# Two old sums fed later: P5 of a blocked matrix product collected in fresh buffers

## The chip, the cores and the metric

One core of one Trainium2 chip runs the whole program. The metric is the device time of one execution in microseconds (us). Before the change it is 2571.3 us, the median of 3 runs (2570.91 to 2572.54). PE is the matrix engine (TensorE), DVE the vector engine, ACT the scalar engine, POOL GpSimd, and SP the engine that only issues DMAs. ACT and POOL issue DMAs too, on queues of their own.

## The reference, cut to what matters

The input x holds 32 items of 128 rows and 2048 features. Of the first layer the part that matters here is one big product: all 4096 rows times one 2048 x 2048 weight (which has the low-rank update already in it). The mixing of an item's 128 rows by its own 128 x 128 matrix, an average of 8 matrices by attention weights, commutes with it and comes after.

```python
agg_w = jnp.einsum('bk,koi->boi', att, weight[..., 0])
out   = jnp.einsum('boi,bih->boh', agg_w, x) + agg_b[:, :, None]
...
out = jnp.einsum('bsd,od->bso', x, W) + bias
upd = jnp.einsum('ebsr,eor,e->bso', einsum('bsd,erd->ebsr', x, A), Bf, coeffs * scales)
x = x + out + upd
```

The second layer (a grouped convolution, a feature permutation, a gated network for each of 16 heads and its inverse permutation) fills the second half of the time and is not touched.

## The kernel before, in words

**The product in three levels.** The big product is done by Strassen's scheme in Winograd's form: a product of 2 x 2 blocks is made of seven products of sums instead of eight. The outer level has the seven rounds `P1, P2, P6, P7, P5, P3, P4`, in this order (`ROUNDS`). A round goes over 8 groups of 4 items, `g` = 0 to 7, so there are 56 steps `(r, g)`, numbered 0 to 55; P5 is steps 32 to 39 and P3 steps 40 to 47. Inside a step the seven products of the second level are again named P1 to P7. One of them is 4 matmuls of 128 x 128 weights and 512 columns that accumulate in one PSUM bank; each 32-bit matmul stands in the trace as two MATMUL records.

**The third level** takes two neighbouring groups (a pair, `PAIRS`) together: for the inner products P2 and P4 of both, 16 matmuls of 512 columns become 28 of 256 (`quarter` in `multiply_third`, all in the odd step of the pair). In the pairs that `MORE` lists, P3 and P7 are done so as well (`multiply_more`, where the first two quarters of each family are in the even step). The weights of the third level are made by POOL and DVE (`third_weights`, `more_weights`), its inputs by POOL or DVE (`third_inputs`: `sq`; `more_inputs`: `sv`).

**What becomes of a product.** A round's products belong to one or two sums in DRAM (`ADDED`). P5 goes to two: `u1` becomes `u3` and `u2` becomes `c11`. `olds_load` loads the old sums one step ahead, DVE adds each PSUM bank to the loaded tile as soon as PE has filled it (`add`, line 600 and line 506; `quarter`, lines 628, 538 and 543), and `part_store` stores the tile from SP's queue after the pair. So in P5 DVE reads each bank twice, once for each sum. Where there is no old sum (P1), the first write to each part of a fresh tile `m_` is a copy by ACT (line 602), and the later ones are DVE's additions.

**What sets the order.** The schedule is written by hand: an engine runs its instructions in the order of the Python calls. `between(j)`, called between the products of a step, puts side work on DVE: `mixed_kernel` (the averages of 8 matrices, lines 725 and 727; `MIXES[r][g]` of them at each of j = 0 to 3), parts of third-level weights (lines 1319 and 1321). Loads of the round's inputs (`x_loads`) and of the next round's weights (`outer_weights`) stand on SP's queue; SP waits, in order, until the place of a load is free, and everything behind that load waits too. POOL makes the sums of inputs (`x_combine`: `pieces`, line 292, then `s`, lines 328 to 331) and, at the end of a round, the next round's inner weights (`inner_weights`, lines 261 to 265).

**Buffers.** All large tiles (128 x 2048, 1 MB) share 26 places (`SLOTS`). A new tile takes a place that another one has left, and the first instruction that writes to it waits for the last one that used the place, which may be a store on another queue. PSUM has 8 banks; a product takes `px` or `py` and reuses it two products later, so PE waits if the bank has not been emptied by then.

Of the kernel before, what the change touches and what calls it, by code (L numbers as in the profile page):

```python
# [11 lines left out]
ALU = mybir.AluOpType  # L12
# [4 lines left out]
P = 128  # L17
B = 32
L = 2048
QW = 512  # L20
# [31 lines left out]
    "P1": (0, 1, 2, 3), "P2": (0, 1, 2, 3), "P6": (0, 1, 2, 3), "P7": (0, 1, 2, 3),  # L52
    "P5": (0, 1, 2, 3), "P3": (0, 1, 2, 3), "P4": (0,),
}
MORE = {"P6": (1,), "P7": (1, 2, 3), "P3": (1, 2, 3)}
MIXES = {
# [6 lines left out]
    "P4": (0,) * 8,  # L63
}
ENDS = ("P1", "P4")
# [4 lines left out]
def adaln_ffn_kernel(  # L70
# [16 lines left out]
    nc = tc.nc  # L87
# [8 lines left out]
    def slot(name, shape=(P, L)):  # L96
        return big.tile(list(shape), FP, name=name, tag="s")


    def bank():  # L100
        return banks.pop(0)
# [178 lines left out]
    def part_load(n, g, shape=(P, 2, 2, QW)):  # L280
        t = slot(f"{n}_{g}", shape)
        nc.sync.dma_start(t.rearrange("p k s c -> p (k s c)"), part_d[n, g])
        return t

    def part_store(n, g, t, eng=nc.gpsimd):
        eng.dma_start(part_d[n, g], t.rearrange("p k s c -> p (k s c)"))
# [30 lines left out]
    def x_combine(r, g, ts):  # L317
# [22 lines left out]
    ADDED = {  # L340
        "P1": [(None, "p1")],
        "P2": [("p1", "c00")],
        "P6": [("p1", "u1")],
        "P7": [("u1", "u2")],
        "P5": [("u1", "u3"), ("u2", "c11")],
        "P4": [("u2", "c10")],
        "P3": [("u3", "c01")],
    }
# [144 lines left out]
    def multiply_more(r, g, lhs, rhs, accs, between, families):  # L493

        px, py = bank(), bank()
        if g % 2 == 0:
            both = [accs]
            held.extend((both, {}, {}))
        both, *sums = held
        if g % 2:  # L500
            both.append(accs)

        def add(ps, *to):
            for si, oi in to:
                for acc in accs:
                    nc.vector.tensor_tensor(acc[:, si, oi], ps, acc[:, si, oi], ALU.add)

        def product(k, ps, first, last):
            for kc in range(4):
                nc.tensor.matmul(  # L510
                    ps, lhsT=lhs[k][:, bass.ts(kc, P)], rhs=rhs[k][kc],
                    start=first and kc == 0, stop=last and kc == 3, skip_group_check=True,
                )

        def quarter(n, k):

            quarters, x = families[n]
            qs = sums[n]
            if k in ("P1", "P5", "P2"):
                qs[k] = bank()  # L520
            ps = qs[{"P6": "P1", "P7": "P1", "P4": "P1", "P3": "P5"}.get(k, k)]
            first, last = k in ("P1", "P2", "P5"), k in ("P2", "P3", "P4")
            for i, out in enumerate(halves(ps)):
                for kc in range(2):
                    nc.tensor.matmul(
                        out, lhsT=x[k][:, 1 - i if n else i, bass.ts(kc, P)],
                        rhs=quarters[i][k][kc],
                        start=first and i == 0 and kc == 0, stop=last and i == 1 and kc == 1,
                        skip_group_check=True,
                    )  # L530
            b, h = {
                "P1": (0, 0), "P2": (0, 0), "P6": (0, 1), "P5": (1, 1), "P7": (1, 1),
                "P3": (0, 1), "P4": (1, 0),
            }[k]
            cols = slice(h * NQ, (h + 1) * NQ)
            for acc in both[b]:
                part = acc[:, :, n, cols]
                nc.vector.tensor_tensor(
                    part, ps.rearrange("p (s n) -> p s n", s=2), part, ALU.add
                )  # L540
                if n:
                    part = acc[:, 1, 0, cols]
                    nc.vector.tensor_tensor(part, ps[:, NQ : 2 * NQ], part, ALU.add)
            if last:
                done(ps)

        def quarters_of(*nks):
            if g % 2:
                for n, k in nks:
                    quarter(n, k)  # L550

        product("P1", px, True, False)
        add(px, (0, 0))
        between(0)
        quarters_of((0, "P6"), (0, "P5"))
        if g % 2:
            sums_rest(nc.vector)
        product("P5", py, True, True)
        add(py, (1, 1), (0, 1))
        done(py)  # L560
        between(1)
        quarters_of((1, "P6"), (0, "P7"))
        product("P6", px, False, True)
        add(px, (0, 1), (1, 1), (1, 0))
        done(px)
        between(2)
        if g % 2 == 0:
            quarter(0, "P1")
            quarter(0, "P2")
            between(3)  # L570
            quarter(1, "P1")
            between(4)
            quarter(1, "P2")
            between(5)
            return
        quarters_of((1, "P5"), (0, "P3"))
        between(3)
        quarters_of((1, "P7"), (0, "P4"))
        between(4)
        quarters_of((1, "P3"))  # L580
        between(5)
        quarters_of((1, "P4"))
        held.clear()
        for b, accs in enumerate(both):
            for (_, new), acc in zip(ADDED[r], accs):
                part_store(new, g - 1 + b, acc, nc.sync)

    def multiply_third(r, g, lhs, rhs, olds, between, quarters, sq):

        px, py = bank(), bank()  # L590
        accs = olds if olds[0] is not None else [slot(f"m_{r}{g}", (P, 2, 2, QW))]
        fresh = set()
        if sq:
            both = [held.pop(), accs]
# [47 lines left out]
                for k, to in turns[n]:  # L642
                    quarter(k, to)

        early = r not in ENDS
        product("P1", px, True, False)
        add(0, 0, px)
        between(0)
# [26 lines left out]
        if not sq:  # L675
            held.append(accs)
            return
        for b, accs in enumerate(both):
            for (_, new), acc in zip(ADDED[r], accs):
                part_store(new, g - 1 + b, acc, nc.scalar if r == "P1" else nc.sync)  # L680

    held = []

    def outer_weights(r, kc):

# [499 lines left out]
    steps = [(r, g) for r in ROUNDS for g in range(NG)]  # L1185
# [40 lines left out]
    olds = {}  # L1226
# [4 lines left out]

    def olds_load(i):
        r, g = steps[i]
        olds[i] = [old and part_load(old, g) for old, _ in ADDED[r]]

    for i, (r, g) in enumerate(steps):
        ri = i // NG
# [18 lines left out]
            olds_load(0)  # L1256
        if i + 1 < len(steps) and not last_round and i != NG - 1:
            olds_load(i + 1)
        ahead = i + 2 < len(steps) and ri > 0 and not last_round
        if ahead and steps[i + 2][0] != "P6":  # L1260
            xs[i + 2] = x_loads(*steps[i + 2])
        if g == NG - (1 if ri else 2) and ri < len(ROUNDS) - 1:
            nxt = inner_weights(ROUNDS[ri + 1], [nxt[kc] for kc in range(4)])
# [40 lines left out]
        def between(j):  # L1304

            if j == 3 and 0 <= k_early < EARLY:
                outer_sums(k_early, early_x)

            b = (ri - 1) * (NG - 2) + g + 1 if ri > 0 else g - (NG - 2)
            if j < 4:  # L1310
                for _ in range(MIXES[r][g]):
                    if mixes:
                        b, k = mixes.pop(0)
                        mixed_kernel(b, (k,))
            if ri == 0 and j == 2:
                for k in blocks[6 + 2 * g : 8 + 2 * g]:
                    wt[k] = w_load(*k)
            if i and j < 4 and quarter_ops:
                nc.vector.tensor_tensor(*quarter_ops.pop(0), ALU.subtract)
            if j < 4 and more_ops:  # L1320
                nc.vector.tensor_tensor(*more_ops.pop(0), ALU.subtract)
            if i == NG - 1 and j == 3:
                olds_load(i + 1)
            if j == 3 and ahead and steps[i + 2][0] == "P6":
                xs[i + 2] = x_loads(*steps[i + 2])
            if ri == 0 and unsummed and (j in (1, 3) and (i, j) != (1, 3) or (i, j) == (3, 2)):
                row_sums(*unsummed.pop())
            if (i, j) in ((2, 5), (3, 0), (3, 4), (4, 0)) and unsummed_first:
                t = unsummed_first.pop(0)
                tt = nc.vector.tensor_tensor  # L1330
                tt(wsum[:, 0, 0], wsum[:, 0, 0], t[:, 0, 0], ALU.add)
                tt(wsum[:, 0], wsum[:, 0], t[:, 1], ALU.add)
            if last_round:
                if j == 1 and i + 1 < len(steps):
                    lhs[i + 1] = x_combine(*steps[i + 1], xs.pop(i + 1))
                    olds_load(i + 1)
                if j == 4 and i + 2 < len(steps):
                    xs[i + 2] = x_loads(*steps[i + 2])
                if j in (2, 4):
                    stage(k0 + j // 2, stage_first)  # L1340
                if j % 2:
                    stage_third(k0 + j // 2)
                else:
                    stage(k0 + j // 2, stage_second)
# [116 lines left out]
```

## Time and profile before

| what | value |
|---|---|
| median of 3 runs | 2571.3 us |
| the profiled execution, by the same clock as the runs | 2569.07 us |
| its span in the profile | 2567.3 us |
| PE busy in the span | 2556.8 us |
| first matmul after the span's start | 1.5 us |
| last matmul's end before the span's end | 5.8 us |
| P5, steps 32 to 39 | 848.5 to 1034.2 us |
| P3, steps 40 to 47 | 1034.2 to 1216.0 us |
| granted TensorE clock | 1.00 |

The profile is a table of what each engine did in one execution. The page sums it up; the timeline lists instructions in order of time, with the idle time ahead of each group in brackets and what ended it; the windows view gives the busy time of each engine in a stretch; the waits view says who waited for whom. A busy PE is not PE at its peak, since matmuls overlap: the distance from one matmul's start to the next is the better measure. The start of a step is the start of its first matmul. Times in the profile count from the start of the span.

### The profile page before, as it was taken

What the parts mean: (1) busy time and instruction counts of PE and PEld (TensorE: products, weight loads), DVE (VectorE), ACT (ScalarE), POOL (GpSimd) and SP (SyncE); (2) the same over time, 40 slices, a digit from 0 to 9 for tenths busy, and PEclk for the clock granted to TensorE, in tenths of its full rate; (3) what the DMA queues carried; (4) which work ended last, traced back from release to release, by engine and by line L of the source; (5) the groups of instructions that cost most, each with busy time, mean ns of one, the idle gap of its engine ahead of it and who ended that gap; (6) DMA issues with size and microseconds to landing.
All of it is one profiled execution on the core that took longest, in us unless ns stands there. A gap on an engine that the chain in (4) does not pass through costs nothing. (4 is left out here: it accounts for less than half of the span.)

```text
span 2567.3 us, 22404 instructions
## 1 busy us (share of the span) xinstructions
PE 2556.8 (100%) x7238; PEld 1373.6 (54%) x7238; DVE 1616.1 (63%) x2505; ACT 532.2 (21%) x1099; POOL 1411.2 (55%) x1170
## 2 busy tenths in 40 slices
PE   9999999999999999999999999999999999999999
PEld 4555555565566555566554455455554554455543
DVE  5575566777776658766477666666666666666601
ACT  0000000000000000000011344444444444444432
POOL 8433677879997836989532144434334434434222
PEclk9999999999999999999999999999999999999999
DMA  8553688569466586574876987777777787787532
GB/s 344 195 187 117 242 322 313 210 267 392 150 248 265 202 340 264 230 287 165 285 237 202 298 297 248 224 251 235 230 218 239 246 251 222 222 250 239 163 125 90
DMA packets 186868, 610.44 MB, mean 238 GB/s; under 512 B 17664, under 2 KB 91904, under 8 KB 142336
## 3 DMA queue, kind: packets, MB, share of 16 engines
q1 hardware_dynamic: 146784, 465.09, 51.0%
q0 software_dynamic: 31264, 119.56, 14.1%
q10 hardware_dynamic: 8704, 24.37, 2.5%
q8 instruction: 58, 0.95, 0.1%
q14 instruction: 58, 0.48, 0.1%
HBM read 372.45 MB, written 202.94 MB: 224 GB/s over the span
## 5 line engine op out<-in xcount | busy, mean ns | idle before, releaser
L999 PE MATMUL bank<-t,ws 128*128 128x512 f32 x1024 | 460.3, 592 | 0.0
L1010 PE MATMUL bank<-gl,ws 128*128 128x512 f32 x1024 | 460.2, 592 | 0.0
L1017 POOL DMA_INDIRECT out<-t,orow x128 | 151.3, 1182 | 545.5 <-DVE t L1015 488.1
L1002 ACT ACTIVATE gl<-bank 128x512 f32<-128x512 f32 x512 | 306.2, 598 | 433.1 <-PE bank L999 430.6
L1010 PEld LDWEIGHTS bank<-gl,ws 128*128 128x128 f32 x1024 | 194.6, 190 | 233.0 <-issue 231.5
L999 PEld LDWEIGHTS bank<-t,ws 128*128 128x128 f32 x1024 | 194.6, 190 | 226.6 <-issue 223.4
L1015 DVE TENSOR_TENSOR t<-bank,t 128x512 f32<-128x512 f32 x128 | 88.4, 690 | 322.0 <-PE bank L1010 322.0
L748 POOL TENSOR_TENSOR x<-x,fb 128x512 f32<-128x512 f32 x128 | 174.2, 1390 | 182.8 <-DMA x<-in_x 133.8
L754 ACT ACTIVATE bank<-w,aggb 128x512 f32<-128x512 f32 x128 | 80.8, 684 | 877.5 <-DMA w<-w_d 865.3
L607 PE MATMUL bank<-P_t,s_P 128*128 128x512 f32 x576 | 255.7, 592 | 0.4 <-ACT m_P L602 0.4
L292 POOL TENSOR_TENSOR xt<-xt,xt 128x512 f32<-128x512 f32 x120 | 156.3, 1334 | 97.7 <-DMA xt<-in_xT 78.8
L727 DVE SCALAR_TENSOR_TENSOR ags<-mix,att_bc,ags 128x128 f32<-128x128 f32 x224 | 200.1, 893 | 4.2
L607 PEld LDWEIGHTS bank<-P_t,s_P 128*128 128x128 f32 x576 | 109.3, 190 | 127.6 <-issue 122.2
L328 POOL TENSOR_TENSOR s_P<-xt 128x512 f32<-128x512 f32 x52 | 68.8, 1323 | 191.4 <-DMA xt<-in_xT 110.3
L983 POOL DMA_INDIRECT t<-hx_d,row x128 | 131.5, 1027 | 54.4 <-issue 25.6
L600 DVE TENSOR_TENSOR u<-bank,u 128x512 f32<-128x512 f32 x132 | 85.3, 685 | 101.9 <-PE bank L607 98.9
L607 PE MATMUL bank<-wo_P,s_P 128*128 128x512 f32 x320 | 142.1, 592 | 0.0
L866 ACT ACTIVATE cv<-bank,ctxb 128x128 f32<-128x128 f32 x256 | 73.0, 368 | 233.4 <-PE bank L855 233.4
L855 PE MATMUL bank<-va,tw_l 128*128 128x256 f32 x512 | 121.1, 379 | 0.0
L766 DVE TENSOR_TENSOR x<-bank,x 128x512 f32<-128x512 f32 x128 | 88.0, 690 | 52.4 <-PE bank L763 21.5
L855 PEld LDWEIGHTS bank<-va,tw_l 128*128 128x128 f32 x512 | 97.0, 190 | 40.9 <-issue 30.5
L600 DVE TENSOR_TENSOR p<-bank,p 128x512 f32<-128x512 f32 x84 | 56.6, 687 | 96.5 <-PE bank L607 94.1
(239 smaller groups left out, 4030.1 us busy)
## 6 DMA issues: line engine op xcount, KB each, us to landing
xt<-in_xT SPq DMA_DIRECT2D x84, 1024.0 KB, 10.3
u<-u_d SPq DMA_DIRECT2D x40, 1024.0 KB, 9.6
wo_P<-wb_d SPq DMA_DIRECT2D x36, 1024.0 KB, 12.3
u<-c_d SPq DMA_DIRECT2D x64, 512.0 KB, 7.0
x<-in_x SPq DMA_DIRECT2D x32, 1024.0 KB, 8.9
xg<-x SPq DMA_DIRECT2D x256, 128.0 KB, 5.1
hx_d<-x1t SPq DMA_DIRECT2D x32, 1024.0 KB, 6.6
hx_d<-ht SPq DMA_DIRECT2D x32, 1024.0 KB, 7.2
```

The lines of the kernel that those rows point to most:

```text
L292: nc.gpsimd.tensor_tensor(out[:, i, j], a[:, i, j], b[:, i, j], op)
L600: nc.vector.tensor_tensor(to, ps, to, ALU.add)
L607: nc.tensor.matmul(ps, lhsT=lhs[k][:, bass.ts(kc, P)], rhs=rhs[k][kc], start=first and kc == 0, stop=last and kc == 3, skip_group_check=True,)
L727: nc.vector.scalar_tensor_tensor(ag, mix[:, k], att, ag, ALU.mult, ALU.add)
L748: nc.gpsimd.tensor_tensor(xt[:, f], xt[:, f], late["fb"][:, f], ALU.add)
L855: nc.tensor.matmul(out, lhsT=w[:, 2 * i + r], rhs=rhs, start=first and r == 0, stop=last and r == 1, skip_group_check=True,)
L983: nc.gpsimd.indirect_dma_start(out=t.rearrange("p k t -> p (k t)"), out_offset=None, in_=hx_d[g].rearrange("l k t -> l (k t)"), in_offset= ...
L999: nc.tensor.matmul(pu, lhsT=w[:, m * P : (m + 1) * P], rhs=t[:, 0], start=True, stop=True)
L1002: nc.scalar.activation(gl[m], pu, AF.Gelu)
L1010: nc.tensor.matmul(pd, lhsT=w[:, (MC + m) * P : (MC + m + 1) * P], rhs=gl[m], start=(m == 0), stop=(m == MC - 1),)
L1015: nc.vector.tensor_tensor(t[:, 1], pd, t[:, 1], ALU.add)
L1017: nc.gpsimd.indirect_dma_start(out=out, out_offset=bass.IndirectOffsetOnAxis(ap=orow[:, g, h : h + 1], axis=0), in_=t[:, 1], in_offset=None,)
```

## The change

P5's results of groups 0 to 5 (three pairs) no longer go to two loaded sums. They are collected in one fresh tile `m_P5g` for each group (first writes by ACT, the others by DVE), and that tile is kept in SBUF. In the next two steps its old sums are loaded and DVE adds the tile to each of them, in halves of 1024 columns at j = 2 to 5 of `between` (line 1345 of the new file, below called a fold); the sums are then stored from ACT's queue. Groups 6 and 7 still go to both sums directly, as before. Pair 1 of P5 (groups 2 and 3) gets the third level for P3 and P7 as well. In a fresh pair the quarters of the odd step come after the products that write the fresh tile first. Loads of P5's inputs are issued later, at j = 3 instead of ahead of the step; P1's stores go from ACT's queue to SP's, but for pair 2; one or two of `MIXES` move between steps, so that P5 has 28 averaging operations instead of 32, and P3 48 instead of 44.

```diff
-MORE = {"P6": (1,), "P7": (1, 2, 3), "P3": (1, 2, 3)}
+MORE = {"P6": (1,), "P7": (1, 2, 3), "P3": (1, 2, 3), "P5": (1,)}
-    "P5": (0, 0, 0, 1, 1, 2, 2, 2),
-    "P3": (0, 2, 1, 2, 1, 2, 2, 1),
+    "P5": (0, 1, 0, 1, 0, 1, 2, 2),
+    "P3": (0, 2, 1, 2, 1, 2, 2, 2),
...
     def multiply_more(r, g, lhs, rhs, accs, between, families):
         px, py = bank(), bank()
+        fresh = accs[0] is None
+        early = not fresh
+        if fresh:
+            accs = [slot(f"m_{r}{g}", (P, 2, 2, QW))]
+        untouched = [(si, oi) for si in range(2) for oi in range(2)] if fresh else []
...
                 for acc in accs:
-                    nc.vector.tensor_tensor(acc[:, si, oi], ps, acc[:, si, oi], ALU.add)
+                    if (si, oi) in untouched:
+                        untouched.remove((si, oi))
+                        nc.scalar.copy(acc[:, si, oi], ps)
+                    else:
+                        nc.vector.tensor_tensor(acc[:, si, oi], ps, acc[:, si, oi], ALU.add)
...
-        quarters_of((0, "P6"), (0, "P5"))
+        quarters_of((0, "P6"), (0, "P5"), now=early)
...
-        quarters_of((1, "P6"), (0, "P7"))
+        quarters_of((1, "P6"), (0, "P7"), now=early)
...
+        quarters_of((0, "P6"), (0, "P5"), (0, "P7"), now=fresh)
+        quarters_of((1, "P6"), now=fresh)
         quarters_of((1, "P5"), (0, "P3"))
...
+        if fresh:
+            folds.extend((g - 1 + b, accs[0]) for b, accs in enumerate(both))
+            return
...
     def multiply_third(r, g, lhs, rhs, olds, between, quarters, sq):
-        early = r not in ENDS
+        early = r not in ENDS and olds[0] is not None
...
+        if r == "P5" and olds[0] is None:
+            folds.extend((g - 1 + b, accs[0]) for b, accs in enumerate(both))
+            return
-                part_store(new, g - 1 + b, acc, nc.scalar if r == "P1" else nc.sync)
+                part_store(new, g - 1 + b, acc, nc.scalar if (r, g) == ("P1", 5) else nc.sync)
...
     def olds_load(i):
-        olds[i] = [old and part_load(old, g) for old, _ in ADDED[r]]
+        olds[i] = [None] if r == "P5" and g < 6 else [old and part_load(old, g) for old, _ in ADDED[r]]
...
+        fold = folds.pop(0) if folds else None
+        if fold:
+            fold += ([part_load(old, fold[0]) for old, _ in ADDED["P5"]],)
         ahead = i + 2 < len(steps) and ri > 0 and not last_round
-        if ahead and steps[i + 2][0] != "P6":
+        if ahead and steps[i + 2][0] not in ("P6", "P5"):
             xs[i + 2] = x_loads(*steps[i + 2])
...
+            if fold and j > 1:
+                n, si = divmod(j - 2, 2)
+                t = fold[2][n]
+                nc.vector.tensor_tensor(t[:, si], t[:, si], fold[1][:, si], ALU.add)
+                if si:
+                    part_store(ADDED["P5"][n][1], fold[0], t, nc.scalar)
...
-            if j == 3 and ahead and steps[i + 2][0] == "P6":
+            if j == 3 and ahead and steps[i + 2][0] in ("P6", "P5"):
                 xs[i + 2] = x_loads(*steps[i + 2])
```

More of the change, by code (lines that the diff above doesn't have):

```diff
@@ L545, in quarter, with quarters_of @@
                 done(ps)
-        def quarters_of(*nks):
-            if g % 2:
+        def quarters_of(*nks, now=True):
+            if g % 2 and now:
                 for n, k in nks:
@@ L677, in multiply_third @@
             return
+        if r == "P5" and olds[0] is None:
+            folds.extend((g - 1 + b, accs[0]) for b, accs in enumerate(both))
+            return
         for b, accs in enumerate(both):
             for (_, new), acc in zip(ADDED[r], accs):
-                part_store(new, g - 1 + b, acc, nc.scalar if r == "P1" else nc.sync)
-    held = []
+                part_store(new, g - 1 + b, acc, nc.scalar if (r, g) == ("P1", 5) else nc.sync)
+    held, folds = [], []
     def outer_weights(r, kc):
```

## The prediction

> **What bounds the kernel now.** I read the page's busy line first, then who PE waits for, then the timeline of PE in P5, and last the busy time step by step. The busy line of the page:
>
> ```profile
> PE 2556.8 (100%) x7238; PEld 1373.6 (54%) x7238; DVE 1616.1 (63%) x2505; ACT 532.2 (21%) x1099; POOL 1411.2 (55%) x1170
> ```
>
> PE is busy nearly throughout. Overlapping matmuls also look busy, so the waits of PE are the next view (us in total, times, longest):
>
> ```profile
> PE bank L166 <- DVE warm L163: 1.5, 1, 1.5
> PE bank L232 <- DVE w L235: 1.3, 1, 1.3
> PE bank L525 <- DVE u L543: 1.0, 2, 0.5
> PE bank L525 <- DVE p L543: 0.4, 1, 0.4
> PE bank L607 <- ACT m_P L602: 0.4, 1, 0.4
> ```
>
> Only three of the five lines are in the rounds, 1.8 us in 2567; line 525 appears where pairs with `MORE` write two sums. Measured on the starts of neighbouring matmuls, all pauses of the run come to 6.4 us, and P5 has none. The timeline of PE in step 34 gives the beat (start, us, operation, count of records):
>
> ```profile
> 894.91 3.60 PE L607 MATMUL bank<-wo_P,xt 128*128 128x512 f32 x8
> 898.34 7.03 PE L607 MATMUL bank<-P_t,s_P 128*128 128x512 f32 x16
> ...
> 922.39 3.62 PE L620 MATMUL bank<-P_q,sq 128*128 128x256 f32 x16
> 925.85 3.60 PE L607 MATMUL bank<-P_t,s_P 128*128 128x512 f32 x8
> ```
>
> From 894.91 to 898.34 are 8 records, so 0.429 us each; a 512-column matmul (two records) costs 0.858 us. Sixteen records of 256 columns fill 922.39 to 925.85, so such a matmul costs 0.432. The busy time in steps 36 to 40 (one line each; per engine):
>
> ```profile
> core 0: us, PE busy (x) PEld busy (x) DVE busy (x) ACT busy (x) POOL busy (x), PEclk, DMA share, GB/s
> 941.30:958.40 17.10, 17.10 (x41) 7.60 (x40) 8.61 (x16) 0.00 (x0) 1.99 (x2) 1.00 0.84 328
> 958.40:987.70 29.30, 29.30 (x97) 18.24 (x96) 25.45 (x34) 0.00 (x0) 22.93 (x19) 1.00 0.75 313
> 987.70:1004.90 17.20, 17.20 (x41) 7.60 (x40) 10.01 (x20) 0.00 (x0) 2.12 (x2) 1.00 0.84 327
> 1004.90:1034.10 29.20, 29.20 (x97) 18.24 (x96) 24.36 (x34) 0.00 (x0) 23.91 (x19) 1.00 0.51 208
> 1034.10:1051.30 17.20, 17.20 (x41) 7.60 (x40) 9.73 (x13) 0.00 (x0) 16.96 (x14) 1.00 0.73 258
> ```
>
> DVE has half of an even step free, but only 4 to 5 us of an odd one. The DMA share is high in steps 36 to 38.
>
> **PE's own work.** Pair 1 of P5 turns 16 matmuls of 512 columns into 28 of 256: 16 x 0.858 - 28 x 0.432 = 13.7 - 12.1, **-1.6 us**. PE is the bound, so this is saved in full if nothing comes late.
>
> **DVE's relief.** Six groups lose their second addition (0.69 us by the row of line 600 below). PE waits for none of them, so this buys **0**. In their place come 24 folds of 1024 columns in SBUF. Their nearest row is line 252:
>
> ```profile
> L252 DVE TENSOR_TENSOR wsum<-wsum,w 128x1024 f32<-128x1024 f32 x24 | 34.6, 1440 | 0.5
> L600 DVE TENSOR_TENSOR u<-bank,u 128x512 f32<-128x512 f32 x132 | 85.3, 685 | 101.9 <-PE bank L607 98.9
> ```
>
> Its shortest is 1.21 us and its longest 2.28. A mix of line 727 takes 0.35 us while POOL rests (999.8 us) and 1.24 while POOL works (1009.8), so I take 1.7 for a fold beside POOL and 1.3 otherwise.
>
> A rule of the Trainium skill (VectorE: DVE Perf Modes, The TRN2 errata) gives such an fp32 addition as (N+151)/0.96 ns, an estimate of 1.22 us for 1024 columns. The shortest row agrees, the mean of 1.44 does not; by the rule the folds named below would end about 0.9 us earlier and the stall of step 37 be 4.4 us instead of 5.4.
>
> **Step 35 (the new `MORE` step).** Ten quarters stand in a row, with folds and mixes on DVE between the evictions. A quarter needs the bank emptied two quarters before; behind two additions, a mix and a fold (about 0.4 + 0.4 + 1.2 + 1.7) one quarter comes some 0.3 late, and later ones like the stalls of line 525 in P3 and P7 (0.2 to 0.7). **+0.7**, between 0 (DVE keeps up, as in P5 now) and 2 (a fold at 2.28 in each of three such places).
>
> **Step 37, where I expect most of it.** Its fresh tile `m_P55` gets the place of `c11`'s sum of group 2 (`u2` loaded in step 36). The last user of that place is the store, now on ACT's queue, that follows the fold at j = 5 of step 36. ACT's first copy into `m_P55` therefore waits for the landing. In the times of before, where step 37 starts at 958.5, and now 1.6 - 0.7 = 0.9 earlier, at 957.6:
> - DVE has added the last bank of step 36 at 957.6 + 0.7 = 958.3, and does the two folds left, 2 x 1.7: 961.7.
> - The store lands. Before, line 286 shows six 1 MB stores from ACT's queue, landing after 3.9 / 10.1 / 12.3 us (least, median, most). At step 37's start SP issues the two loads of 1 MB for the next fold. A second 1 MB transfer of a burst lands 2.1 to 2.5 us after the first, so with one and a half of them mixed in: 3.9 + 1.5 x 2.4 = 7.5. Landing 969.2.
> - The copy, 0.59 to 0.7 with its wake-up: 969.9.
> - PE's third product (P6) takes the bank of the first again two products after the step's start: 957.6 + 16 x 0.429 = 964.5.
>
> So PE stands for **+5.4**. Lower end: folds of 1.2 and a landing in 3.9 give 958.3 + 2.4 + 3.9 + 0.7 = 965.3, 0.8 us. Upper end: a landing in 12.3 gives 10.2. Behind the waiting copy ACT has the other copies and the stores of the next folds; DVE waits for the bank too, so the whole step moves. The other fresh tiles of the even and odd steps have the same kind of predecessor, but 1 us or more to spare by the same working (`m_P54` about 4, `m_P53` about 1): 0, or up to 2, which the upper end covers.
>
> A rule that speaks against this edit is in DMA: Bandwidth & Descriptors, Queues, rings and completion order: an engine goes round-robin between queue rows, so ACT's store would share with SP's loads rather than pass them. The rows of 10.1 and 12.3 us agree; half of 425 GB/s for 1 MB and the page's fixed 2 us make an estimate of 7 us, and the sum would be 0.5 less.
>
> **Steps 38 to 40.** Groups 6 and 7 are still added twice, and the folds of groups 4 and 5 now come on top: step 38 has 10.0 + 4 x 1.4 = 15.6 of 17.2 us, or with POOL's overlap up to 19; step 39 has 24.4 + 4 x 1.5 = 30.4 of 29.3, and mixes that move there. DVE then enters P3 some 8 us behind at worst, and the third product of step 40 waits for the eviction of the first, about 1.9. A second path ends at the same place: P3's inner weights (lines 261 to 265, POOL) need places that a fold's store now frees. `P3_t1` had 4.8 us to spare, `P3_q0` 2.7, `s_P31` 6.1, and the load of `s2_0` stands on SP behind a store from ACT; by these the weights come 0.2 us late. Both are one wait, not two: **+2.0**, between 0 (folds at 1.2 and additions kept inside the free 5 us) and 4 (the backlog and the late load one behind the other).
>
> **The rest.** P3's group 7 has four more mixes, 4 x 0.9 on a DVE that makes line 525 wait: **+0.3**, between 0 and 1.2. The later loads of P5's inputs take from a margin of 20 us before POOL needs them: 0, or at most 1. P1's stores pass to SP's queue, where SP is ahead of their readers by 30 us: 0; should loads stand behind them it is a stall of P1 like that of line 602, 0.4. Four mixes less in P5: 0, DVE has free time there.
>
> **Sum.** -1.6 + 0.7 + 5.4 + 2.0 + 0.3 = **+6.8 us**. Against the profiled execution's own 2569.07 us (span 2567.3) that is 2575.9; it stands 2.2 below the median, so on the median of 2571.3 I forecast **2578.1**.
>
> **Rivals.**
> 1. *Not slower: the store lands alone* (2571.5). If SP's two loads are themselves held by an occupied place, nothing shares the transfers; the store takes 3.9, step 37 loses 0.8, and the rest 1.0 (half of step 35, a third of P3's start): 2571.3 - 1.6 + 0.8 + 1.0. For it: the least row, 3.9, and the fact that the 26 places are all taken. Against: a DMA share of 0.84. It decides once the landing takes under about 5.8 us, since then the whole is below the 5.1 us that count.
> 2. *Only PE's count shows* (2569.7): the folds fit the gaps of DVE (0.95 to 1.74 us in its timeline of step 38) and the store's place is free in time; the relief of DVE does nothing, because PE did not wait for it. For it: no stall in P5 now. Against: odd steps have only 4 to 5 us free.
> 3. *Much slower* (2584): step 37 at its upper end, 10.2 - 5.4 = 4.8 more, and 1 more at P3's start.
> 4. *Faster*: would need the 1.6 and most of the 6.4 us of all pauses, of which only one kind (0.4 at P1's copy) touches what is edited: at best 2563.
>
> **Chances.** Forecast mechanism from 2576.4 up to 2582: 0.42; rival 3: 0.08; rival 1: 0.31; rival 2: 0.17; rival 4: 0.02. Differences of under 0.2% (5.1 us) are about what a measurement of this kernel can't tell from no change. So slower by more than that 0.50, the same 0.48, faster 0.02. The range runs from rival 2 (2569.4, with its 0.3 of scatter) to rival 3 (2586, its mechanism with 2 us of the other fresh tiles), leaving out about 1 in 10.
>
> **What would show it.** Right: 7 to 10 us of new pauses of PE, most of it one wait for ACT's first copy (line 513 or 616 of the new file) at the start of step 37, with a landing of 6 to 10 us in the row of the folds' stores (line 286), and a smaller one in the first products of P3. The distance from step 34 to 36 should shrink by 1.6 less any stall. Wrong: no wait for ACT at step 37 with landings near 4 (rival 1 or 2); a stall in P1 or elsewhere in P2 to P7, which I cost at nothing; folds of 1.2 us beside POOL, which take away the terms of steps 35 and 40.

## The result, and the profile after

The changed kernel takes **2581.57 us** (median of 6, 2580.89 to 2583.44) against 2571.11 for the kernel before (median of 6): ratio 1.0043, 95% interval 1.0033 to 1.0053, so 10.5 us slower. The profiled execution took 2580.89 us with a span of 2578.7, 11.4 more than the 2567.3 of before. The forecast was 2578.1 with a range of 2569.4 to 2586.0.

The page's busy line, and then who PE waited for (us in total, times, longest), in the changed kernel (line 513 or 616 is ACT's first copy, 534 a quarter of the third level, 621 a product):

```profile
PE 2559.4 (99%) x7262; PEld 1378.7 (53%) x7262; DVE 1625.7 (63%) x2470; ACT 545.9 (21%) x1123; POOL 1443.3 (56%) x1182
```

```profile
PE bank L621 <- POOL P_t L261: 5.4, 2, 3.3
PE bank L621 <- ACT m_P L616: 3.2, 3, 2.1
PE bank L534 <- DVE u L552: 1.6, 2, 0.9
...
PE bank L519 <- ACT m_P L513: 0.6, 1, 0.6
```

The busy line hides it all: PE is at 99% instead of 100%. The waits show three new ones in P5 and P3 (0.4 of the 3.2 is P1's copy, as before), and the largest is not the one that the forecast put first: 5.4 us for POOL's sums for P3's inner weights. Worked out as before, on the starts of neighbouring matmuls:

| part | us |
|---|---|
| 16 matmuls of 512 columns become 28 of 256 | -1.6 |
| step 35: third product 0.9, one quarter 0.3 | +1.2 |
| step 36, third product | +0.9 |
| step 37, third product | +2.3 |
| step 40, second product of P3: two waits 6.2, then matmuls at half speed 3.2 | +9.4 |
| the pause at 178 us is gone | -1.5 |
| new small pauses at 353 us (0.3) and 1413 us (0.9, layer two) | +1.2 |
| sum, against 11.4 in the span | +11.9 |

What the sum has too much lies in small pauses that are not listed: one of 0.4 us at 756 us is gone, the start is 0.2 us shorter, and one at 800 us is 0.2 us longer.

The steps say the same: from the start of step 34 to that of step 36 it took 46.42 us before and 45.98 now (-1.6 + 1.2), step 37 took 29.26 and now 31.56, step 40 took 17.16 and now 26.62.

**Steps 35 to 37.** The timeline of ACT in the changed kernel (start, us, operation; in brackets the idle time ahead and what ended it):

```profile
916.83 0.33 ACTq L286 DMA_DIRECT2D c_d<-u  x1
917.26 1.56 ACT L513 COPY m_P<-bank 128x512 f32<-128x512 f32 x3 [11.64 <-DVE ags L742]
...
946.09 1.07 ACT L616 COPY m_P<-bank 128x512 f32<-128x512 f32 x2 [22.41 <-DMA u_d<-u]
...
961.45 0.33 ACTq L286 DMA_DIRECT2D c_d<-u  x1
965.56 1.07 ACT L616 COPY m_P<-bank 128x512 f32<-128x512 f32 x2 [6.86 <-DMA c_d<-u]
```

The last two lines are the predicted wait of step 37: the store of `c11`'s sum of group 2 is issued at 961.45, lands 4.0 us later, and the copy into `m_P55` starts 0.1 us after that. In step 36 it is the same with the store of group 1's first sum, which landed 9.8 us after its issue. In step 35 the copy starts right behind the issue of a store on ACT itself.

**P3's start.** The timeline of SP's queue in the changed kernel:

```profile
1015.47 0.32 SPq L282 DMA_DIRECT2D s<-s_d  x1
```

The same load in the kernel before:

```profile
994.67 0.65 SPq L282 DMA_DIRECT2D s<-s_d  x1
```

What POOL waited for between 1000 and 1050 us in the changed kernel:

```profile
POOL xt L292 <- DMA s<-s_d: 17.1, 1, 17.1
```

The load of `s2_0`, which P3's first step needs, was issued at 994.67 before and now at 1015.47: its place is that of `u1`'s old sum of group 4, whose store went out at 1007.75 and landed at 1015.33. POOL stood still for 17.1 us until the load landed (18.6 us before, where the load came sooner), began P3's sums at 1020.59 (1008.46 before) and then had all of P3's inner weights to make. The timeline of PE shows the price, and the windows the clock:

```profile
1038.61 1.88 PE L621 MATMUL bank<-P_t,s_P 128*128 128x512 f32 x4
1043.78 2.07 PE L621 MATMUL bank<-P_t,s_P 128*128 128x512 f32 x2 [3.29 <-POOL P_t L261]
1048.00 7.09 PE L621 MATMUL bank<-P_t,s_P 128*128 128x512 f32 x10 [2.15 <-POOL P_t L261]
```

```profile
core 0: us, PE busy (x) PEld busy (x) DVE busy (x) ACT busy (x) POOL busy (x), PEclk, DMA share, GB/s
1043.00:1048.00 5.00, 2.07 (x2) 0.50 (x2) 1.27 (x2) 0.00 (x0) 4.79 (x4) 0.50 1.01 397
1048.00:1053.00 5.00, 5.00 (x6) 2.17 (x7) 2.29 (x2) 0.00 (x0) 4.89 (x4) 0.50 1.01 411
```

The third part of the weights comes 3.3 us late and the fourth 2.2 us more; after the first wait the granted clock is 0.50 in these windows, and a record takes 0.85 us instead of 0.43. POOL, too, was slower than before while it made them (lines of POOL, then of DVE):

```profile
1034.40 2.33 POOL L263 TENSOR_TENSOR P_t<-wo_P,P_t 128x512 f32<-128x512 f32 x1
```

```profile
1034.39 1.21 DVE L1345 TENSOR_TENSOR u<-u,m_P 128x1024 f32<-128x1024 f32 x1
```

A sum of POOL that starts together with a fold of DVE takes 2.33 us instead of 1.27. From the start of POOL's chain to the weights' fourth part it took 27.4 us (24.4 before); four such sums beside folds and one beside line 1339 make 4.3 of it (before, POOL also waited 1.1 us in this stretch). The Trainium skill (SBUF — State Buffer, Who interferes with whom) says that a DVE instruction with two SBUF inputs and a GpSimd instruction that reads SBUF exclude each other, the later one waiting for the earlier. The rows agree: 2.33 is 1.27 and most of a fold's 1.21.

### The profile page after: what moved, and what is told of

It reads as the page before. It is cut to its first block, busy times and chain, and to the rows that moved or that the text cites. A ratio compares the mean times of both kernels' runs of the same rounds, so it can differ in the third digit from the quotient of the medians.

```text
span 2578.7 us, 22472 instructions
## 1 busy us (share of the span) xinstructions
PE 2559.4 (99%) x7262; PEld 1378.7 (53%) x7262; DVE 1625.7 (63%) x2470; ACT 545.9 (21%) x1123; POOL 1443.3 (56%) x1182
## 5 line engine op out<-in xcount | busy, mean ns | idle before, releaser
L621 PE MATMUL bank<-P_t,s_P 128*128 128x512 f32 x544 | 245.5, 600 | 8.6 <-POOL P_t L261 5.4
L744 DVE SCALAR_TENSOR_TENSOR ags<-mix,att_bc,ags 128x128 f32<-128x128 f32 x224 | 212.6, 949 | 4.3
L616 ACT COPY m_P<-bank 128x512 f32<-128x512 f32 x48 | 27.8, 586 | 757.6 <-PE bank L621 626.9
L621 PEld LDWEIGHTS bank<-P_t,s_P 128*128 128x128 f32 x544 | 104.1, 192 | 134.2 <-issue 120.0
L621 PE MATMUL bank<-wo_P,s_P 128*128 128x512 f32 x288 | 127.5, 592 | 0.0
L780 PE MATMUL bank<-u,agl 128*128 128x512 f32 x256 | 115.1, 592 | 0.0
```

The source lines that it names most:

```text
L621: nc.tensor.matmul(ps, lhsT=lhs[k][:, bass.ts(kc, P)], rhs=rhs[k][kc], start=first and kc == 0, stop=last and kc == 3, skip_group_check=True,)
L744: nc.vector.scalar_tensor_tensor(ag, mix[:, k], att, ag, ALU.mult, ALU.add)
L780: nc.tensor.matmul(pm, lhsT=ag, rhs=u[:, f], start=False, stop=True, skip_group_check=True)
```

## The experiments

Each ran beside the kernel before on the same chip. The median of before was 2571.08 for experiments 1 to 4, 2571.01 for 5 to 8 and 2570.35 for 9 to 12. In the diffs "..." stands for lines left out, and a line in round brackets for several lines that it sums up.

**1. Pair 2 directly**

```diff
-        olds[i] = [None] if r == "P5" and g < 6 else ...
+        olds[i] = [None] if r == "P5" and g < 4 else ...
```

> The changed kernel, but groups 4 and 5 go directly to both old sums again, as groups 6 and 7 do; groups 0 to 3 stay fresh. Theory A (the folds of groups 4 and 5 and their stores from ACT's queue cause the wait at step 37 and the late start of P3): the pause of 2.2 us at step 37's third product and the 9.4 us in the first products of P3 both go, the pauses in steps 35 and 36 (1.2 and 0.9) stay: 2581.6 - 11.7 = 2569.9 us. Theory B (the later loads of P5's inputs and the moved mixes delay POOL, the folds do not): P3's pause stays at 7 us or more, 2577 to 2580 us.

Measured: 2585.51 us, ratio 1.0055 (1.0041 to 1.0069). The two pauses did go (none in step 37's third product, 1.1 us left at P3's start), as theory A said. But PE had lost 13 us by then, which gave POOL time as well, so this run alone does not show that the folds of groups 4 and 5 made them, and theory B is not ruled out by it; experiments 5, 8, 10 and 12 bear on that. The new pause of 13.2 us, slow matmuls behind it included, stands in step 35, and smaller ones in steps 37, 39 and 41 (0.7, 1.5 and 1.8). Step 35, PE, then ACT, each from its own timeline:

```profile
931.12 6.25 PE L519 MATMUL bank<-P_t,s_P 128*128 128x512 f32 x8 [10.39 <-ACT m_P L513]
```

```profile
920.24 0.36 ACTq L286 DMA_DIRECT2D c_d<-u  x1
930.39 1.56 ACT L513 COPY m_P<-bank 128x512 f32<-128x512 f32 x3 [21.39 <-DMA c_d<-u]
```

The old sums of group 4, now loaded here, took two places, and the fresh tile `m_P53` got the place of a sum whose store was just going out; among the loads it took 10 us to land. It is the predicted mechanism of step 37 at its upper end, in another step. My expectation had counted the places as they were; when one tile goes, the others get other places.

**2. and 4. Two parts alone, on the kernel before**

```diff
-MORE = {"P6": (1,), "P7": (1, 2, 3), "P3": (1, 2, 3)}
+MORE = {"P6": (1,), "P7": (1, 2, 3), "P3": (1, 2, 3), "P5": (1,)}
```

> The kernel before, with the third level for P3 and P7 in P5's pair 1, and nothing else of the change: both old sums are added directly, no fresh tiles, no folds. Theory A (the fresh tiles cost more than the double additions did): step 35 pauses like the pairs of P7 and P3 that write two sums, 0.5 to 1.5 us in all, against the 1.6 saved: 2570 to 2571 us, no worse than before. Theory C (with ten quarters in a row DVE can't keep up with two sums, so the fresh tiles are needed for this pair): pauses of 3 us or more in step 35, 2573 us or more.

Measured: 2572.31 us, ratio 1.0006 (0.9997 to 1.0015). The one pause in step 35 is 1.3 us, within theory A's 0.5 to 1.5; the time is 1.3 us above what I expected (the profiled execution also paused 1.2 us at 171 us and 1.0 at 1404, which before does not), and the interval does not tell it from the kernel before. Theory C's 3 us are not there.

```diff
-                part_store(new, g - 1 + b, acc, nc.scalar if r == "P1" else nc.sync)
+                part_store(new, g - 1 + b, acc, nc.scalar if (r, g) == ("P1", 5) else nc.sync)
```

> The kernel before, with P1's stores on SP's queue except group pair 2's, and nothing else of the change. In the changed kernel the 1.4 us pause at 178.3 us (PE waits for DVE, line 235 of before) is gone. If the moved stores did that: 2571.1 - 1.4 = 2569.7 us and no pause near 178. If not, 2571.1 us, and the pause is there or comes and goes; if loads behind the stores come late, a new pause of P1's products and more than 2571.5 us.

Measured: 2570.90 us, ratio 1.0000 (0.9991 to 1.0009). The pause at 178 us is gone, but small ones stand at 37 us (0.7), 354 us (0.3) and 1401 us (0.8): no gain in the time.

**3. P3's inputs ahead of the fold's sums**

```diff
-        (loads of the fold's old sums)
         if ahead and steps[i + 2][0] not in ("P6", "P5"):
             xs[i + 2] = x_loads(*steps[i + 2])
+        (loads of the fold's old sums)
```

> The changed kernel, but at the start of a step the loads of the inputs two steps ahead are issued before the loads of the fold's old sums, so that the first input of P3 gets a place before the sums of group 4 do. Theory A (P3 starts late because this load waits for the place of a sum whose store from ACT lands late): the load is issued before 992 us, POOL's sums for P3 start by 1006 instead of 1020.6, and P3's pause falls from 9.4 us to under 1.5; some of it comes back as DVE waiting for the later fold loads in step 38 (0 to 4 us): 2572 to 2576 us. Theory D (the folds' additions slow POOL beside them, and that makes the weights late): the pause stays at 4 us or more, 2577 us or more.

Measured: 2592.59 us, ratio 1.0086 (1.0072 to 1.0099). POOL began P3's sums at 1004.7, as theory A said, but DVE then waited 11.4 us for the sum of group 4, which now had the late place, and with it PE 11.8 us in step 39, where I had allowed 4 (DVE's timeline, then PE's):

```profile
1014.55 1.57 DVE L1345 TENSOR_TENSOR u<-u,m_P 128x1024 f32<-128x1024 f32 x1 [11.43 <-DMA u<-u_d]
```

```profile
1028.81 6.01 PE L634 MATMUL bank<-P_q,sq 128*128 128x256 f32 x16 [11.75 <-DVE u L642]
```

P3 still paused 5.3 us, which by the bounds set is theory D's side: POOL had made the sums of P3's inputs by 1019.7 and then waited until 1041.8 for a place for the weights, and four of its later sums were slow (1.7 to 2.3 us). The load itself went out at 999.8, not before 992.

**5. The fresh tile first.** In groups 0 to 5 the loads are issued after the first product's copy:

```diff
+        deferred = r == "P5" and g < 6
+        def loads():
+            (loads of old sums, of the fold's sums, of outer weights, of inputs)
+        if not deferred:
+            loads()
...
         def between(j):
+            if j == 0 and deferred:
+                loads()
```

> The changed kernel, but in the steps with a fresh tile (groups 0 to 5) the loads of the step (old sums, the fold's sums, the next round's weights) are issued after the first product's copy, so that the fresh tile gets the first free place and a load gets the place behind the fold's store. Theory A (PE waits in steps 35 to 37 because the copy into the fresh tile waits for a fold or for the landing of its store): the pauses of 0.9, 0.9 and 2.3 us at the third products of steps 35, 36 and 37 go; P3's pause of 9.4 us stays, or grows by up to 3 because the first sum of group 4 now has its place 2.5 us later: 2577.5 to 2580.5 us. Rival (the pauses come from ACT or DVE being late themselves): the three pauses stay, 2581 us or more.

Measured: 2579.65 us, ratio 1.0035 (1.0021 to 1.0048). The pauses of steps 36 and 37 are gone: the place was their cause. That of step 35 grew from 0.9 to 1.9 us, though the place of `m_P53` was free by then: in experiment 9, with the same places, the copy started at 916.2 instead of 920.9. For this one the theory failed, and the rival (ACT itself is late) stood. P3's pause was 8.4 us.

**9. The store behind the copy.** As 5, with the same places, but the store that follows a step's last fold is issued after the next step's first copy:

```diff
         def loads():
+            if deferred and kept:
+                part_store(*kept.pop(0))
...
-                    part_store(ADDED["P5"][n][1], fold[0], t, nc.scalar)
+                    to = (ADDED["P5"][n][1], fold[0], t, nc.scalar)
+                    if n and g < 5:
+                        kept.append(to)
+                    else:
+                        part_store(*to)
```

> As the kernel with the fresh tile first (2579.65 us, where step 35 still paused 1.9 us at its third product although the fresh tile's place had long been free), but the store behind a step's last fold is issued on ACT behind the next step's first copy instead of ahead of it; all places stay the same. Theory F (ACT is in order: the copy stands behind the store, and the store waits for DVE's last fold): the pause in step 35 goes from 1.9 us to 0.2 or less: 2577.5 to 2578.5 us. Rival (the copy waits for something else, for instance DVE's additions to the other bank): the pause stays, 2579.7 us.

Measured: 2577.77 us, ratio 1.0029 (1.0018 to 1.0040), and step 35 has no pause at its third product (ACT's timeline):

```profile
916.17 0.58 ACT L513 COPY m_P<-bank 128x512 f32<-128x512 f32 x1 [8.31 <-PE bank L519]
918.76 0.35 ACTq L286 DMA_DIRECT2D c_d<-u  x1
```

The copy now waits for PE's bank alone, and the store, which waits for DVE's fold, comes 2.6 us later. So the pause in step 35 was a queue: the copy stood behind a store that stood behind a fold.

**8. Fold's sums ahead, folds earlier.** As 5, and:

```diff
+            (loads of the fold's old sums ahead of olds_load for g < 7)
-            if fold and j > 1:
-                n, si = divmod(j - 2, 2)
+            j0 = 2 * (g % 2)
+            if fold and j0 <= j < j0 + 4:
+                n, si = divmod(j - j0, 2)
```

> As the kernel with the fresh tile first, and besides the fold's old sums are loaded ahead of the next group's old sums, and in the even steps the folds stand at j = 0 to 3 instead of 2 to 5, so that in step 38 the store of the first folded sum goes out some 8 us earlier and the first inputs of P3 get their places earlier. Theory A (P3 starts late because of those places): the first input of P3 is loaded by 1013 us instead of 1020.4, P3's pause falls from 9.4 us to between 0 and 3, the pauses of steps 35 to 37 stay gone: 2568.5 to 2572 us. Theory D (the additions of the folds slow POOL and DVE in steps 38 and 39, whatever the places do): P3's pause stays at 5 us or more, 2573.5 us or more.

Measured: 2575.83 us, ratio 1.0022 (1.0013 to 1.0031). POOL began P3's sums at 1015.2 instead of 1020.6 and P3's pause fell from 9.4 to 5.4 us. The earlier start came with 4 us less of a pause, but by the bounds set this is theory D's side: in this chain, too, four of POOL's sums took 2.1 to 2.3 us. A pause of 2.0 us came in step 38, where DVE's folds now stand between products.

**10. and 12. What delays P3's weights.**

```diff
-                nc.vector.tensor_tensor(t[:, si], t[:, si], fold[1][:, si], ALU.add)
+                if fold[0] != 5:
+                    nc.vector.tensor_tensor(t[:, si], t[:, si], fold[1][:, si], ALU.add)
```

> The changed kernel without DVE's four additions of group 5's folds in step 39 (loads and stores of those sums stay; P5's part of group 5 is missing from both sums). Theory D (POOL's sums for P3's weights take 2.1 to 2.3 us instead of 1.27 beside such an addition, four of them, 4.0 us on the chain that PE waits for): POOL's sums between 1020 and 1048 us all take 1.3 us but those beside line 1339, P3's pause falls from 9.4 us to 2 to 4: 2574 to 2576 us. Theory A alone (only the late load counts): P3's pause stays at 8 us or more, 2580.5 us or more.

```diff
-            fold += ([part_load(old, fold[0]) for old, _ in ADDED["P5"]],)
+            fold += ([fold[1] if (old, fold[0]) == ("u1", 4) else part_load(old, fold[0]) for old, _ in ADDED["P5"]],)
...
+                if t is not fold[1]:
...
```

> The changed kernel without the load of the first old sum of group 4 and the two additions to it (the fresh tile itself is stored in its stead, so that sum lacks its old part). One place and 1 MB of load fewer in step 38; the additions of group 5 beside POOL stay. Theory A (the first input of P3 waits for the place of that sum): it is issued by 1007 instead of 1015.5 us, POOL's sums for P3 start by 1013 instead of 1020.6, and P3's pause falls from 9.4 us to between 0 and 2: 2572 to 2574.5 us. Theory D alone (slow POOL whatever the places): the pause stays at 4 us or more, 2576 us or more.

Measured: without group 5's additions 2572.15 us, ratio 1.0007 (0.9997 to 1.0016); without the sum of group 4 2578.19 us, ratio 1.0030 (1.0020 to 1.0040). In both POOL starts P3's sums at nearly the same time, 23.0 and 22.6 us ahead of step 40 (14.6 in the changed kernel, 25.7 before). Without the additions P3 does not pause at all; with them the pause is 6.6 us. (The profiled execution without the additions paused 5.0 us in step 37, matmuls at half speed included, instead of 2.3.) The weights' part in the timeline of POOL, first the kernel without group 4's sum:

```profile
1029.46 1.27 POOL L261 TENSOR_TENSOR P_t<-wo_P 128x512 f32<-128x512 f32 x1 [4.07 <-PE bank L634]
...
1036.44 2.34 POOL L262 TENSOR_TENSOR P_t<-wo_P,P_t 128x512 f32<-128x512 f32 x1
```

then the kernel without group 5's additions:

```profile
1026.57 1.28 POOL L261 TENSOR_TENSOR P_t<-wo_P 128x512 f32<-128x512 f32 x1 [0.97 <-PE bank L621]
...
1034.01 1.27 POOL L262 TENSOR_TENSOR P_t<-wo_P,P_t 128x512 f32<-128x512 f32 x1
```

With the load early, the weights' own place is the next late thing (4.07 us until PE's last quarter that reads it), and then POOL is slow beside the folds (three sums of 2.1 to 2.3 us). By the bounds set, experiment 12 is on theory D's side, and experiment 10 fell below what either theory gave. Both expectations had treated the load and the slow sums as one or the other. The early load alone leaves 6.6 us of the pause; where it is early and the slow sums are gone too, the pause is gone. No run has the late load without the slow sums. Dropping the additions also changes the places (the load went out at 1008.7, and the weights waited less for theirs: 0.97 and 2.24 us against 4.07 and 1.74), so how much of the 9.4 us each of the three holds by itself is not separated.

**6. Filling the wait.** Seven more matmuls of the first product go into a free bank:

```diff
             for kc in range(4):
+                if (r, g, k) == ("P3", 0, "P5") and kc > 1:
+                    fill = banks[0]
+                    for n in range(6 - kc):
+                        nc.tensor.matmul(
+                            fill, lhsT=lhs["P1"][:, bass.ts(n, P)], rhs=rhs["P1"][n],
...
```

> The changed kernel with 7 more matmuls of 512 columns (6.0 us of PE work, results not used) put where PE waits in P3's second product, 4 ahead of its third part and 3 ahead of its fourth. They do not hasten POOL's weights. Theory E (after PE stood still for 3.3 us its granted clock is halved for some 9 us, and that is 2.6 us of the loss behind the last wait): the granted clock stays at 1.00, the matmuls behind keep 0.43 us, and the kernel is 2.6 us faster than the changed kernel in spite of the added work: 2579 us. Rival (the slow matmuls have to do with the weights or with memory traffic): they stay slow, 2581.6 us or more.

Measured: 2582.29 us, ratio 1.0049 (1.0033 to 1.0064). The windows of this kernel, to be held against 0.50 above:

```profile
1043.00:1048.00 5.00, 4.63 (x11) 1.82 (x10) 2.85 (x3) 0.00 (x0) 4.84 (x4) 1.00 1.05 374
1048.00:1053.00 5.00, 4.46 (x11) 1.82 (x10) 1.44 (x2) 0.00 (x0) 4.84 (x5) 1.00 0.97 359
```

The clock stays at 1.00, and step 40 takes 24.6 us instead of 26.6. But step 41 then waits 1.6 us for POOL (line 411), which it did not in the changed kernel; steps 40 and 41 together take 55.79 against 55.88. So theory E was right on the clock and wrong on the 2.6 us: POOL's chain sets the end of these two steps, and what PE gains in the one it waits for in the other.

**7. and 11. Without fresh tiles.** On experiment 2:

```diff
-    "P5": (0, 0, 0, 1, 1, 2, 2, 2),
+    "P5": (0, 1, 0, 0, 1, 2, 2, 2),
```

> The kernel before with the third level for P3 and P7 in P5's pair 1 and both sums added directly (as the earlier run), and the averaging operations of P5 moved: none in group 3's step, four more in group 1's. The earlier run paused 1.3 us in that step. If DVE's averages between the quarters make that pause: it goes, and 2569.5 to 2570.5 us, the first version below the kernel before. If the double additions alone make it: it stays at 1 us or more, 2571 to 2572.5 us.

Measured: 2570.16 us, ratio 0.9999 (0.9990 to 1.0008). The pause in step 35 is 0.2 us instead of 1.3, so the averages between the quarters made most of it; the time cannot be told from before.

And with experiment 4's line as well:

> The kernel before with the third level for P3 and P7 in P5's pair 1 added directly to both sums, the averages moved out of group 3's step (2570.16 us in its run), and P1's stores on SP's queue except pair 2's. If the stores' move takes away the 1.4 us pause at 178 us and gives nothing back: 2569 us, below the kernel before by about 0.08%. If, as when it was moved alone, the pauses only change their places: 2570.2 us.

Measured: **2568.18 us**, ratio 0.9991 (0.9982 to 1.0000), 2.2 us below the kernel before, where the changed kernel was 10.5 above. All its pauses come to 6.1 us, none at 178 us; who PE waited for in it:

```profile
PE bank L525 <- DVE u L543: 1.9, 3, 0.8
PE bank L166 <- DVE warm L163: 1.5, 1, 1.5
PE bank L607 <- ACT m_P L602: 0.4, 1, 0.4
PE bank L525 <- DVE p L543: 0.4, 1, 0.4
```

These are the kinds of before, and the wait for ACT, POOL or a landing is gone from P5 and P3. The interval ends at 1.0000, so a gain is likely but not quite shown; of the 28 executions of before, only one was as fast as the slowest of this kernel's 11. The 2.2 us fit the 1.6 us of matmuls and the 0.3 us less of pauses, but are not separated into them.

## Why the prediction was right, and where not

The kernel became slower, as forecast, and by the kind of cause that was forecast: PE waits for work that stands behind the place of a stored sum. That the total came within 3.5 us is in part luck. The forecast put 5.4 of its 8.4 us of new waits on step 37 and 2.0 on P3's start; it was 2.3 and 9.4, and the two errors have opposite signs. By its own signs of being right (7 to 10 us of new pauses, most of it in step 37, with a landing of 6 to 10 us) it was wrong: 13.8 us, most of it at P3's start, and 4.0 us.

- **What bounds the kernel, and PE's -1.6:** right. Step 34 to 36 shortened by 1.6 less the pauses.
- **DVE's relief at 0:** right. With the double additions kept and the averages moved (experiments 7 and 11), PE pauses 0.2 us in step 35. P5 had no pause that the relief could remove.
- **Duration of a fold:** 24 of them took 1.21 to 2.29 us, median 1.22 instead of the 1.3 and 1.7 taken. The page's formula (1.22 us) that was weighed against the trace is the typical fold; the long ones are those beside POOL.
- **Step 35, +0.7, measured 1.2:** the quarter was 0.3 late as said, the other 0.9 has another cause than the one given: ACT's order (experiment 9), not a row of late quarters.
- **Step 36, 0 with 4 us to spare, measured 0.9:** the same mechanism as step 37; the store landed 9.8 us after its issue, and five loads were issued around it, between 935 and 940 us. That they made it late was not tested.
- **Step 37, +5.4, measured 2.3:** the mechanism was right to the store and the copy (experiment 5), and the fold's end (961.4, forecast 961.7) too. The landing was mis-sized: 4.0 us, not 7.5. SP's two loads were not beside it; they waited for places until 965.5, as rival 1 had it. That rival's condition came true, but its total did not, because of P3's start. (The gaps of DVE that rival 2 gives for step 38, 0.95 to 1.74 us, reach into step 39; in step 38 its timeline has 0.59 to 1.57.)
- **Steps 38 to 40, +2.0 with an upper end of 4, measured 9.4:** this is the step that failed. It took the load behind ACT's store as 0.2 us late, by margins of before; the load went out 20.8 us later than before. It did not count that POOL would be slowed by the folds (4.3 us in its chain), though the row of line 727 (0.35 and 1.24 us) showed the same contact from DVE's side; and it knew nothing of the halved clock (3.2 us of the 9.4; by experiment 6 steps 40 and 41 together would have been no shorter without it). The path that it priced first, DVE's backlog at the third product of step 40, does not show: both waits of step 40 are for POOL, in the second product. The reason "both are one wait, not two" made the term small. In POOL's chain the late start and the slow sums stand one behind the other, and the early start alone (experiment 12) leaves 6.6 us.
- **P3's group 7, +0.3, measured 1.2 there and 0.1 in P3:** the end of step 47, group 7, now has a pause of 1.2 us at line 534, where before had none. The pauses of steps 43 and 45 (0.3 and 0.8) are gone in turn, why is not known, so P3's pauses of this kind come to 1.2 us instead of 1.1. **P1's stores:** no effect by themselves (experiment 4).

The sum was 3.5 us short: one term 3.1 too large, one 7.4 too small, and smaller ones.

## What to carry to other kernels

A result that is kept to be added later needs a place, and so do the sums that it waits for. When all places are taken, look at who gets the place behind each store: a store's landing (4 to 10 us here) on the place of a fresh tile or of a next stage's input can become a wait of the engine that bounds the kernel, and taking one tile away can move the wait instead of removing it (experiments 1 and 3). Before a stage's work is spread to other engines, ask whether the engine that bounds it waited for that work at all: in P5 it never did, and the plain version with direct additions (experiment 11) was the only one measured below the kernel before by more than 1 us.

## What was not expected of the hardware

- After a wait of 3.3 us the granted TensorE clock was 0.50 and stayed there for about 9 us, in which a second wait of 2.2 us lies; after the wait of 2.1 us in step 37 it stayed at 1.00. In other runs it went to 0.50 after waits of 3.0 (experiment 10, step 37) to 3.5 us (experiment 8, where it was back at 1.00 some 3 us later), and stayed at 1.00 after one of 3.0 (experiment 3, step 37). The Trainium skill (TensorE: Matmul & The Clock Gate, What's actually happening) states half rate after an idle window of some 3.4 us that runs freely. The rows agree that the same length of wait can end either way, but here waits from 3.0 us on were enough. With the wait filled by matmuls the clock stayed at 1.00 (experiment 6).
- A 128 x 512 sum of POOL that meets a 128 x 1024 sum of DVE from SBUF takes 2.1 to 2.3 us instead of 1.27, and a fold beside POOL up to 2.29 instead of 1.21.
